# An attention and feed-forward kernel on one core: projection products split into four column groups of TensorE

## The chip, the cores and the metric

The kernel runs on one core of a Trainium2 chip. The core has TensorE (matrix products, PE in the profile; its weight loads are the row PEld), VectorE (DVE), ScalarE (ACT), GpSimd (POOL) and SyncE (SP), which issues most of the transfers. Each runs its own list of instructions, and they wait for each other by semaphores. The metric is the time of one execution on the device in microseconds (us), the median of several runs.

## The reference, cut to what matters

Four sequences of 1024 tokens with 512 channels go through cross-attention and a quantised feed-forward block, each behind a layer norm and added to its input:

```python
x = x + xattn(layernorm(x), ctx, Wq, bq, Wk, bk, Wv, bv, Wo, bo, 256, 768)
x = x + ffn(layernorm(x), clip_x, clip_down, w_gate, w_up, w_down)
# xattn: 16 heads of 32 channels
qh, kh, vh = heads(q @ Wq + bq), heads(kv @ Wk + bk), heads(kv @ Wv + bv)
scores = einsum('bhqd,bhkd->bhqk', qh, kh) * 32 ** -0.5
out = einsum('bhqk,bhkd->bhqd', softmax(where(mask, scores, -inf)), vh)
return merge(out) @ Wo + bo
```

The mask has three image chunks of 256 tokens that attend to themselves alone, and a text chunk of 256 tokens that attends to all image tokens and causally to itself. The change concerns the four products with Wq, Wk, Wv and Wo, which are 512x512 float32 matrices.

## The kernel before, in words

**Tiling.** The tokens of each sequence are cut into four blocks of 256 (`QB`), 16 blocks in all. Channels stand in four chunks of 128 partitions (`NCC`), and four heads of 32 channels share a chunk. A unit of attention is one block of queries, one chunk of heads (`g`), and one block of keys; an image block has one key block, a text block has four.

**The projections.** A `Job` makes the queries, or the keys and values, of one block. `rows` (L276) multiplies 128 columns of Wq or Wk, the stationary operand, by the transposed input `self.T` of 256 tokens, the moving operand, and sums over four chunks of the contraction in PSUM; it does this for two output chunks, `a`. ScalarE then moves the result with its bias to Q or K (L279). The values (L318) have 128 tokens of `self.T` as stationary operand and 512 columns of Wv as moving operand. `Output.step` (L603) multiplies 128 tokens of the attention output `oT` by 512 columns of Wo in the same way, and VectorE adds the result to the input (L582). Each call of one of these is a run of matmuls on TensorE that nothing else of TensorE interrupts. Near the end (`LATE`) some runs are made in halves. Line 288, the first block's keys, and line 777, the last block's output, are products of the same kind that have their own code.

**The attention.** `maxima` makes the scores (L421 image, L432 text), 32 rows of the array for each head; `weights` makes them again transposed, with the maximum subtracted by a small bfloat16 product (L479, L484); `values` multiplies the exponentials by V (L523) and by ones (L541), 32 columns of the array for each head:

```python
nc.tensor.matmul(
    av[rows_of(j), 0, cols], va[:, n, g * P + j * D : g * P + (j + 1) * D], u.pT[:, j, n, cols],
    start=..., stop=..., tile_position=(0, j * D), skip_group_check=True,
)
```

So the kernel already uses TensorE's array in three ways: whole (128 rows by 128 columns), as four row groups (32 rows by 128 columns), and as four column groups (128 rows by 32 columns).

**The order.** The attention phase runs under a hand-written order. In step `n` of the loop at L812 stand `maxima` of unit n, then one piece of projection or output work (`large`, L829), then `weights` of unit n-5 and `values` of unit n-6; where there is no such piece, `values` comes ahead of `weights`. A second piece of projection may follow at L879, at the end of the step. Semaphores are set by the framework from what each instruction reads and writes.

**Float32.** Each float32 matmul of the program is two passes in the profile, each a weight load and a matmul. The program has 5391 matmuls on TensorE; the profile has 9179 records of matmuls and 9201 of weight loads. The feed-forward part (L1038, L1129, L1141) has bfloat16 products of one pass.

Of the kernel before, what the change touches and what calls it, by code (L numbers as in the profile page):

```python
# [19 lines left out]
P = 128  # L20
B, N, C = 4, 1024, 512
NH, D = 16, 32
FF = 1408
NCC = C // P
# [18 lines left out]
def kernel(ctx: ExitStack, tc: tile.TileContext, x, kv, Wq, bq, Wk, bk, Wv, bv, Wo, bo, clip_x, clip_down, w_gate, w_up, w_down, out):  # L43
    nc = tc.nc
# [77 lines left out]
    with ExitStack() as actx:  # L122
# [35 lines left out]
        W = {name: p.tile([P, NCC, C], F32, tag=name, name=f"{name}_sb") for name, p in (("Wo", ap), ("Wk", wp), ("Wv", wp), ("Wq", wp))}  # L158

        idle = ps_mm.tile([P, 512], F32, tag="mm", name="idle")  # L160
        rhs = onesb.unsqueeze(1).to_broadcast([P, 4, P])
# [51 lines left out]

        early = [True]

        def bank(name):

            if early[0]:
                return ps_sc.tile([P, 2, 2, QB], F32, tag="sc", name=name).rearrange("p a b c -> p a (b c)")[:, 0, :]
            return ps_mm.tile([P, 512], F32, tag="mm", name=name)  # L220
# [16 lines left out]
        class Job:  # L237
# [8 lines left out]
            def run_small(self):  # L246
                if self.small == 0:
                    self.T = wk2.tile([P, NCC, QB], F32, tag="tT", name=f"{self.kind}T_{self.c}")
                i = self.small
                self.small += 1  # L250
                if self.c > 0:
                    src = spreads.pop(self.a)
                    nc.vector.transpose(self.T.rearrange("p c (k q) -> p k c q", q=D), src.rearrange("p k (e c) -> p k c e", c=NCC))
                    return

                if self.kind == "q":
                    while not ready.get(self.c):
                        background.popleft()()
                src = cb0 if self.kind == "kv" else xb0
                pt = bank(f"pt_{self.kind}_{self.c}_{i}").rearrange("p (a b) -> p a b", a=NCC)  # L260
                cols = src[:, i, :].rearrange("p (f k) -> p k f", k=NCC)
                for cc in range(NCC):
                    nc.tensor.transpose(pt[:, cc, :], cols[:, cc, :], ident)
                nc.scalar.copy(self.T[:, :, i * P : (i + 1) * P], pt)
                if i == 1 and self.kind == "kv":
                    columns_of_biases()
                elif i == 1:
                    next_queries(self.c)

            def rows(self, dst, w, b, scale, co, parts):  # L270

                pk = bank(f"pp_{self.kind}_{self.c}_{co}_{parts[0]}").rearrange("p (a q) -> p a q", a=2)
                for a in parts:
                    for ci in range(NCC):
                        lhs = W[w][:, ci, (co + a) * P : (co + a + 1) * P]
                        nc.tensor.matmul(pk[:, a, :], lhs, self.T[:, ci, :], start=(ci == 0), stop=(ci == NCC - 1))  # L276
                for a in parts:
                    bias = bqk[:, b + co + a : b + co + a + 1]
                    nc.scalar.activation(dst[:, co + a, :], pk[:, a, :], AF.Identity, bias=bias, scale=scale)  # L279
# [18 lines left out]
            def run_big(self, half=False):  # L298

                parts = (self.part,) if half or self.part else (0, 1)  # L300
                c, i = self.c, self.big
                first = parts[0] == 0
                if self.kind == "q":
                    if i == 0 and first:
                        Q[c] = qp.tile([P, NCC, QB], F32, tag="qT", name=f"qT_{c}")
                    self.rows(Q[c], "Wq", 0, QK_SCALE, 2 * i, parts)
                elif i < 2:
                    if i == 0 and first:
                        K[c] = kp.tile([P, NCC, QB], F32, tag="kT", name=f"kT_{c}")
                    self.rows(K[c], "Wk", NCC, 1.0, 2 * i, parts)  # L310
                else:
                    i -= 2
                    if i == 0 and first:
                        V[c] = kp.tile([P, 2, C], F32, tag="va", name=f"va_{c}")
                    cols = slice(parts[0] * QB, (parts[-1] + 1) * QB)
                    pv = bank(f"pv_{c}_{i}_{parts[0]}")
                    for ci in range(NCC):
                        nc.tensor.matmul(pv[:, cols], self.T[:, ci, i * P : (i + 1) * P], W["Wv"][:, ci, cols], start=(ci == 0), stop=(ci == NCC - 1))  # L318
                    nc.scalar.copy(V[c][:, i, cols], pv[:, cols])
                if parts[-1] == 1:  # L320
                    self.big += 1
                    self.part = 0
                else:
                    self.part = 1
                return len(parts)
# [56 lines left out]
        def rows_of(j):  # L382
            return slice(j * D, (j + 1) * D)
# [179 lines left out]
        class Output:  # L563
# [34 lines left out]
            def step(self, half=False):  # L598
                i = self.i
                cols = slice(self.part * QB, (self.part + 1) * QB) if half or self.part else slice(0, C)  # L600
                po = ps_mm.tile([P, 512], F32, tag="mm", name=f"po_{self.k.n}_{i}_{self.part}")
                for cc in range(NCC):
                    nc.tensor.matmul(po[:, cols], self.k.oT[:, cc, i * P : (i + 1) * P], W["Wo"][:, cc, cols], start=(cc == 0), stop=(cc == NCC - 1))  # L603
                statistics = self.take(po, i, cols)
                if statistics is None:
                    self.part = 1
                else:
                    background.appendleft(statistics)
                    self.part = 0
                    self.i += 1  # L610
# [287 lines left out]
        for i in range(2):  # L898
            cols = slice(i * P, (i + 1) * P)
# [298 lines left out]
```

## Time and profile before

| | |
|---|---|
| median of 3 runs | 1147.1 us (1145.67 to 1147.92) |
| the profiled execution | 1145.78 us, of which the span from first to last instruction is 1144.1 us |
| granted TensorE clock | 0.993 of full speed |
| TensorE busy | 1123.2 us, 98% of the span |
| weight loads busy | 655.7 us, 57% |
| VectorE, ScalarE, GpSimd busy | 784.0, 500.3, 549.3 us |
| matmul records of L276, L318, L603 | 992, 272, 280 |
| code fetched for TensorE (queue q8) | 72 packets of 16 KB |

The page of the profile gives the busy time of each engine, then the chain of work that ended last, followed back from the last instruction, then groups of instructions by line. A row such as `L276 PE MATMUL pp_q<-qT,Wq_sb 128*128 128x256 f32 x512 | 121.8, 390` reads: line 276, on TensorE, writes pp_q from qT and Wq_sb, 128 rows by 128 columns of the array, moving operand of 128x256 float32, 512 records, 121.8 us busy in all, 390 ns the mean of one. Matmuls overlap each other, so a mean of 390 ns is a time from start to end and not the spacing of two matmuls. In the timeline a row is a group of records in a row: its start, the time to the end of its last one, and their number.

### The profile page before, as it was taken

How to read it: one execution, taken by the hardware profiler on the slowest of the kernel's cores; microseconds unless marked ns; L12 is line 12 of the kernel's file. 1: busy time of each engine (PE TensorE's matmuls, PEld its weight loads, DVE VectorE, ACT ScalarE, POOL GpSimd, SP SyncE). 2: the span in 40 equal slices, each digit the busy share in tenths (PEclk: the TensorE clock that was granted, in tenths of full speed). 3: DMA queues.
4: the chain of work that ended last, by engine and by line, in shares of the span. 5: the costliest groups of instructions: out<-in, count | busy, mean ns of one | idle time of the engine just before them, and what ended most of it. 6: DMA issues, size and time to landing. Idle time of an engine off the chain costs nothing.

```text
span 1144.1 us, 22086 instructions
## 1 busy us (share of the span) xinstructions
PE 1123.2 (98%) x9179; PEld 655.7 (57%) x9201; DVE 784.0 (69%) x979; ACT 500.3 (44%) x700; POOL 549.3 (48%) x618
## 2 busy tenths in 40 slices
PE   9999999999999999999999999998999899999998
PEld 6666656575656656665646566665664344444344
DVE  2546676766577857567777656775676688877887
ACT  3334433343444434444433345544343466553553
POOL 1224546567664567775546569566763222110110
PEclk9999999999999999999999999999999899999999
DMA  7342213123222221331323122110222499310895
GB/s 257 111 127 63 61 48 101 48 85 92 80 61 75 73 78 57 92 114 24 86 66 86 40 73 79 46 50 26 85 67 75 133 282 292 80 38 11 303 388 191
DMA packets 117165, 118.50 MB, mean 104 GB/s; under 512 B 55548, under 2 KB 86536, under 8 KB 115656
## 3 DMA queue, kind: packets, MB, share of 16 engines
q1 hardware_dynamic: 111104, 83.26, 26.0%
q0 software_dynamic: 5648, 33.30, 7.8%
q8 instruction: 72, 1.18, 0.4%
q10 hardware_dynamic: 312, 0.53, 0.2%
q14 instruction: 29, 0.24, 0.1%
HBM read 71.57 MB, written 33.29 MB: 92 GB/s over the span
## 4 chain that ended last, share of the span: by engine, by line
PE 94%; DVE 2%; POOL 2%; ACT 1%; issue 1%; DMA 0%; DVEq 0%; POOLq 0%; ACTq 0%
PE pv L318 10%; PE po L603 10%; PE pp_q L276 10%; PE pp_kv L276 10%; PE av L523 9%; PE t L484 8%; PE pg L1038 7%; PE pu L1038 6%; PE s L432 6%; PE pd L1141 5%; PE s L421 5%; PE t L479 3%; PE av L541 3%; POOL sp L509 1%; PE pd L1129 1%
## 5 line engine op out<-in xcount | busy, mean ns | idle before, releaser
L489 ACT ACTIVATE pT<-t 128x1024 f32<-128x1024 f32 x224 | 217.1, 1021 | 193.8 <-PE t L484 186.4
L509 POOL TENSOR_TENSOR sp<-sp,pT 128x1024 f32<-128x1024 f32 x86 | 190.4, 2214 | 40.9 <-ACT pT L489 37.1
L443 DVE TENSOR_REDUCE nmh<-s 128x2 f32<-128x1024 f32 (+1 forms) x128 | 145.3, 1157 | 71.1 <-PE s L432 68.9
L509 POOL TENSOR_TENSOR sp<-pT 128x1024 f32<-128x1024 f32 x59 | 138.8, 2352 | 92.6 <-ACT pT L489 92.5
L425 DVE TENSOR_REDUCE nmh<-s 128x4 f32<-128x1024 f32 x96 | 112.7, 1215 | 101.2 <-PE s L421 101.2
L276 PE MATMUL pp_q<-qT,Wq_sb 128*128 128x256 f32 x512 | 121.8, 390 | 0.0
L318 PE MATMUL pv<-Wv_sb,kvT 128*128 128x512 f32 (+1 forms) x272 | 118.8, 579 | 0.0
L523 PE MATMUL av<-pT,va 128*32 128x256 f32 (+1 forms) x1792 | 116.5, 377 | 1.0 <-ACT avs L886 1.0
L484 PE MATMUL t<-qT,kT 32*128 32x256 f32 (+1 forms) x1792 | 113.0, 366 | 0.0
L603 PE MATMUL po<-Wo_sb,oT 128*128 128x512 f32 (+1 forms) x280 | 112.5, 544 | 0.2
L276 PE MATMUL pp_kv<-kvT,Wk_sb 128*128 128x256 f32 x480 | 111.5, 385 | 0.0
L556 DVE RECIPROCAL avs<-avs 128x256 f32<-128x256 f32 x63 | 109.8, 1742 | 0.0
L276 PEld LDWEIGHTS pp_q<-qT,Wq_sb 128*128 128x128 f32 x512 | 95.5, 192 | 23.1 <-issue 7.9
L276 PEld LDWEIGHTS pp_kv<-kvT,Wk_sb 128*128 128x128 f32 x480 | 88.8, 190 | 20.5 <-issue 7.6
L557 POOL TENSOR_TENSOR oT<-avs 128x256 f32<-128x256 f32 x63 | 46.0, 731 | 99.6 <-DVE avs L556 99.5
L484 PEld LDWEIGHTS t<-qT,kT 32*128 32x128 f32 x1792 | 88.1, 184 | 6.8
L1038 PE MATMUL pg<-xqT,wgT 128*128 128x512 bf16 x344 | 89.9, 381 | 1.1 <-DVE xqT L999 0.5
L1038 PE MATMUL pu<-xqT,wuT 128*128 128x512 bf16 x345 | 89.7, 380 | 0.4
L1044 ACT ACTIVATE silu<-pg,sg 128x512 f32<-128x512 f32 x88 | 60.0, 687 | 64.7 <-PE pg L1038 62.7
L1065 DVE SCALAR_TENSOR_TENSOR h<-pu,su,silu 128x512 f32<-128x512 f32 x88 | 65.4, 747 | 30.1 <-PE pu L1038 27.4
L318 PEld LDWEIGHTS pv<-Wv_sb,kvT 128*128 128x128 f32 x272 | 49.0, 189 | 54.4 <-issue 50.0
L432 PE MATMUL s<-kT,qT 32*128 32x256 f32 (+1 forms) x1024 | 76.3, 387 | 3.0 <-ACT pT L489 3.0
(186 smaller groups left out, 1415.3 us busy)
## 6 DMA issues: line engine op xcount, KB each, us to landing
xt<-x_d SPq DMA_DIRECT2D x16, 1024.0 KB, 6.3
h<-h_d POOLq DMA_DIRECT2D x3, 2816.0 KB, 13.4
xb<-in_x_dram SPq DMA_DIRECT2D x16, 512.0 KB, 3.8
xr<-in_x_dram SPq DMA_DIRECT2D x16, 512.0 KB, 3.8
x_d<-xr POOLq DMA_DIRECT2D x16, 512.0 KB, 3.8
spread_kv<-in_ctx_dram SPq DMA_DIRECT2D x60, 128.0 KB, 2.6
xn_d<-xb SPq DMA_DIRECT2D x15, 512.0 KB, 3.2
spread_q<-xn_d SPq DMA_DIRECT2D x60, 128.0 KB, 2.7
```

What stands on the lines that cost most here:

```text
L276: nc.tensor.matmul(pk[:, a, :], lhs, self.T[:, ci, :], start=(ci == 0), stop=(ci == NCC - 1))
L318: nc.tensor.matmul(pv[:, cols], self.T[:, ci, i * P : (i + 1) * P], W["Wv"][:, ci, cols], start=(ci == 0), stop=(ci == NCC - 1))
L425: nc.vector.tensor_reduce(nmh[:, h, :, :, 0], prs[h], AX.X, ALU.max, negate=True)
L432: nc.tensor.matmul(prs[j // 2][:, j % 2, kk, :w], q[rows_of(j), g, i * P : (i + 1) * P], K[k.keys[2 * half + kk]][rows_of(j), g, :w], star ...
L443: nc.vector.tensor_reduce(nmh[:, h, :, i, half], s[:, :, :n], AX.X, ALU.max, negate=True)
L484: nc.tensor.matmul(prs[j // 2][:, j % 2, n, cols], kc[rows_of(j), g, n * P : (n + 1) * P], q[rows_of(j), g, cols], start=False, stop=(n == 1))
L489: nc.scalar.activation(pT[:, 2 * h : 2 * h + 2], prs[h], AF.Exp)
L509: nc.gpsimd.tensor_tensor(sp[:, :, cols], a, pT[:, :, n, cols], ALU.add)
L523: nc.tensor.matmul(av[rows_of(j), 0, cols], va[:, n, g * P + j * D : g * P + (j + 1) * D], u.pT[:, j, n, cols], start=(u.part == 0 and n = ...
L556: nc.vector.reciprocal(avs[:, 1, :], avs[:, 1, :])
L603: nc.tensor.matmul(po[:, cols], self.k.oT[:, cc, i * P : (i + 1) * P], W["Wo"][:, cc, cols], start=(cc == 0), stop=(cc == NCC - 1))
L1038: nc.tensor.matmul(ps, w[:, cc, ic * P : (ic + 1) * P], qT[:, cc, :], start=(cc == 0), stop=(cc == NCC - 1))
```

## The change

A new function `column_groups` replaces one matmul of 128 stationary columns by four of 32, each at its own column group of the array and with its own 32 partitions of the result. Lines 276, 318 and 603 call it; lines 288, 198 and 777 stay as they are. The lines after 215 move by seven.

```diff
+        def column_groups(out, lhs, rhs, start, stop):
+
+            for j in range(4):
+                nc.tensor.matmul(
+                    out[rows_of(j)], lhs[:, rows_of(j)], rhs, start=start, stop=stop, tile_position=(0, j * D), skip_group_check=True
+                )
+
...
-                        nc.tensor.matmul(pk[:, a, :], lhs, self.T[:, ci, :], start=(ci == 0), stop=(ci == NCC - 1))
+                        column_groups(pk[:, a, :], lhs, self.T[:, ci, :], ci == 0, ci == NCC - 1)
...
-                        nc.tensor.matmul(pv[:, cols], self.T[:, ci, i * P : (i + 1) * P], W["Wv"][:, ci, cols], start=(ci == 0), stop=(ci == NCC - 1))
+                        column_groups(pv[:, cols], self.T[:, ci, i * P : (i + 1) * P], W["Wv"][:, ci, cols], ci == 0, ci == NCC - 1)
...
-                    nc.tensor.matmul(po[:, cols], self.k.oT[:, cc, i * P : (i + 1) * P], W["Wo"][:, cc, cols], start=(cc == 0), stop=(cc == NCC - 1))
+                    column_groups(po[:, cols], self.k.oT[:, cc, i * P : (i + 1) * P], W["Wo"][:, cc, cols], cc == 0, cc == NCC - 1)
```

The program then has 7707 matmuls on TensorE where it had 5391. The order of the work on every engine is the same.

## The prediction

> **What bounds the kernel now.** I read the engines' busy times first, then the chain of work that ended last, both on the page.
>
> ```profile
> PE 1123.2 (98%) x9179; PEld 655.7 (57%) x9201; DVE 784.0 (69%) x979; ACT 500.3 (44%) x700; POOL 549.3 (48%) x618
> PE 94%; DVE 2%; POOL 2%; ACT 1%; issue 1%; DMA 0%; DVEq 0%; POOLq 0%; ACTq 0%
> ```
>
> TensorE is the bound: 94% of the chain is its own work, and the next engine is busy 69%. A microsecond of TensorE is a microsecond of the end. But busy time does not say how fast its passes follow each other, so I went on to the groups by shape, and then to the timeline of one step.
>
> ```profile
> L276 PE MATMUL pp_q<-qT,Wq_sb 128*128 128x256 f32 x512 | 121.8, 390 | 0.0
> L523 PE MATMUL av<-pT,va 128*32 128x256 f32 x1664 | 113.0, 385 | 1.0 <-ACT avs L886 1.0
> L276 PEld LDWEIGHTS pp_q<-qT,Wq_sb 128*128 128x128 f32 x512 | 95.5, 192 | 23.1 <-issue 7.9 <-ACT pT L489 0.8 <-DVE avs L556 0.8
> L523 PEld LDWEIGHTS av<-pT,va 128*32 128x32 f32 x1792 | 46.7, 109 | 54.6 <-issue 23.3 <-ACT kT L279 3.7 <-ACT qT L279 3.3
> ```
>
> These hold both forms: the product as it is (L276, 128 columns), and the form it is to have, in use already for the values (L523, 32 columns, at the same width of 256). One pass lasts as long in either, 390 and 385 ns. A weight load is 192 ns for 128 columns and 109 ns for 32.
>
> ```profile
> 298.27 3.72 PE L276 MATMUL pp_kv<-kvT,Wk_sb 128*128 128x256 f32 x16
> 301.92 0.39 PE L479 MATMUL t<-nmT,onesb 2*128 2x512 bf16 x4
> 302.15 1.03 PE L484 MATMUL t<-qT,kT 32*128 32x256 f32 x16
> 303.11 1.07 PE L523 MATMUL av<-pT,va 128*32 128x256 f32 x16
> 304.00 0.61 PE L541 MATMUL av<-sp,ones 128*32 128x256 f32 x8
> 304.54 1.15 PE L421 MATMUL s<-kT,qT 32*128 32x256 f32 x16
> 305.62 1.55 PE L603 MATMUL po<-Wo_sb,oT 128*128 128x512 f32 x3
> ```
>
> Starts minus starts give real costs. L541 has 8 records in 0.54 us: two sets of four that run at once in the four groups, 0.216 each, and 0.11 to drain before L421. L523 has 16 records in 0.89 us: four sets of 0.216 and 0.024 more. L276 has 16 records, one at a time, in 3.65 us: 16 x 0.216 is 3.456, and 0.194 is left. In the single records, 0.104 of that is between the first pass and the second (320 ns apart, all later ones 216), while the first weight load isn't covered; 0.09 to 0.10 is the drain at the end, before L479 with its other use of the array. So a set of four 32-column passes costs what one 128-column pass costs, and the two forms differ only at the ends of a run.
>
> **The change, part by part.**
>
> *Steady part.* The 992 records of L276, 272 of L318 and 280 of L603 become sets of four. The sets cost 0.216 us at width 256, as L523 shows. At width 512 the trace has no 32-column float32 pass: between 0.43 (twice L523's; the wide pass at L603 has 0.43 too) and four in turn, 1.7 us. I take 0.43, since L479's four 512-wide passes start within 10 ns of each other. Change: 0.
>
> *Start of a run.* Coming from row groups, the second pass follows with 0.104 us more than its spacing (113 runs in the trace, all 101 to 155 ns), because a load of 190 ns stands open. With 32 columns it is 0.024 (L523). Gain 0.080 a run.
>
> *End of a run.* The four passes of a set start over 20 ns (7 ns apart in L523's records), so the last ends 20 ns later. The drain is 0.112 behind a column-group run (L541 to L421) and 0.093 to 0.096 behind a wide one. Loss 0.02 a run. Net 0.06 us for each run between row groups; the trace has 112, together 6.7 us.
>
> *A change of mode that goes away.* In 18 runs the projection comes right behind `values`, which is in column groups already:
>
> ```profile
> 200.67 0.61 PE L523 MATMUL av<-pT,va 128*32 128x256 f32 x8
> 201.22 3.72 PE L276 MATMUL pp_kv<-kvT,Wk_sb 128*128 128x256 f32 x16
> 204.87 0.94 PE L432 MATMUL s<-kT,qT 32*128 32x256 f32 x16
> ```
>
> Two sets need 0.43, and L276 starts after 0.55: a drain of 0.113. Then 0.104 for the first load. Both go, as between L523 and L541, which follow each other in the same spacing. Less 0.02 at the end: 0.2 x 18 = 3.6 us. The four other runs stand at the start between wide ones or elsewhere: nothing.
>
> *Instructions.* 2316 more float32 matmuls are 4632 more weight loads and as many passes on TensorE, 9264 on 18,380. Their code is 0.59 MB on the 1.18 MB of q8, which arrives in 16 KB packets (256 instructions), one in 13 us now and one in about 7 us in a step with L276; a packet takes 0.9 to 1.4 us, so the fetch stays hidden if it runs ahead at all. What is not free is their issue. A step with L276 is 7.14 us (291.20 to 298.34 in the chain), and will hold 64 + 60 pairs of load and pass, 248 instructions: 28.8 ns each. Now they come at half that rate, with the queue filling during each wide run. How fast can the sequencer feed? The trace bounds it twice. First, the densest stretch:
>
> ```profile
> 717.65 0.39 PE L479 MATMUL t<-nmT,onesb 2*128 2x512 bf16 x4
> 717.88 1.03 PE L484 MATMUL t<-qT,kT 32*128 32x256 f32 x16
> 718.84 0.86 PE L523 MATMUL av<-pT,va 128*32 128x256 f32 x16
> 719.51 0.61 PE L541 MATMUL av<-sp,ones 128*32 128x256 f32 x8
> 719.94 0.83 PE L541 MATMUL av<-pT,ones 128*32 128x256 f32 x16
> 720.71 1.15 PE L432 MATMUL s<-kT,qT 32*128 32x256 f32 x16
> ```
>
> 76 pairs in 3.83 us (to the last start), with no gap but the drains. At L1141 a semaphore wait of TensorE's sequencer is recorded 16 loads ahead of the array, so some 34 of the 152 instructions were queued before, and the rest came in at 32 ns or faster. Second, at 7.8 us the queue is empty: the sequencer ends one recorded wait at 7.779, issues two loads and two passes (L183), and begins its next wait at 7.894. Four in 115 ns is 29 ns at most; two waits with nothing between them elsewhere are 54 to 60 ns apart, so the four took some 15 each. I take 15, and keep 29 to 31 as the slow end.
>
> [...]
>
> *Other engines.* Their instructions and order are the same. ScalarE's moves (L279, L319) and VectorE's add (L582) start up to 0.06 earlier. TensorE's semaphore waits as separate instructions rise from 60 to 79, each 51 ns of the sequencer, behind a queue some 16 pairs deep: nothing; without that cover, 19 x 0.11 = 2 us.
>
> Sum: 6.7 + 3.6 = 10.3 us. Against the profiled execution 1145.8 - 10.3 = 1135.5. The median of the runs stands 1.3 us above that execution, so 1136.8.
>
> **The rivals.**
>
> *The sequencer becomes the bound (slower).* Place: the steps with L276, with eight instructions for each 0.216 us. It decides above 28.8 ns an instruction. For it: at 7.80 the first load and the first pass behind an empty queue are 31 ns apart. At 31 ns a step is 7.69, 0.55 us more than now; 62 of them lose 34 us, the other runs (about 72, half the extra density because they are 512 wide) still gain some 6: 1175 us. At 29.5 ns it would be about even. Against it: the 115 ns above.
>
> *The four groups don't run at once.* In all column-group rows of before the four moving operands differ; here they are one. If reading it together cost even a tenth, the 427 us of these lines (1104 passes of 0.216, 440 of 0.43) would grow by 43: 1180. Against it: L523 reads four streams over all 128 partitions already.
>
> *The gain is hidden.* If TensorE came to wait for others as much earlier as it gets ahead, 1147. For it: four waits of TensorE's sequencer between 730 and 804 us end 30 ns after VectorE's signal. Against it: TensorE had 0.55 to 1.06 us of queued work each time.
>
> **How the numbers follow.** My forecast has 0.73, with 1132 to 1142 of its own: the low end if the exit cost is also smaller, the high end if half the gain per run is lost. The hidden gain has 0.06, the sequencer as bound 0.14 (half of that only mildly, below 1165), the groups in each other's way 0.07. The range is 1132 to 1165, which takes in forecast, hidden gain and a mild bound. A change below 0.2% (2.3 us) can't be told from none. Faster by more 0.74, within 0.06, slower 0.20.
>
> **What would show it.** Right: sets of L276 and L318 0.216 and 0.43 apart, the second set 24 ns late and not 104, no drain between L523 and a following projection, runs of 3.59 us where they were 3.65. Wrong: sets of L276 further apart than 0.216 towards a run's end, or steps of more than 7.14 us, which is the sequencer; a pass of the split lines longer than 0.38 us, or the second to fourth of a set starting late, which is the shared operand; gaps ahead of L421 or L432 that name VectorE, which is the hidden gain.

## The result, and the profile after

The changed kernel takes 1139.43 us, the median of four runs (1138.92 to 1140.27), against 1146.89 us (1145.67 to 1147.92) for the kernel before. The ratio is 0.9936, with a 95% interval from 0.9919 to 0.9953. That is 7.5 us less; the forecast was 10.3 less. The profiled execution took 1139.15 us with a span of 1137.4, against 1145.78 and 1144.1, which is 6.6 us less. All lines behind 215 have moved by seven: L219 is the matmul of the new function, L428 and L439 are the scores, L486 and L491 the transposed scores, L530 and L548 the products with V and with ones.

From the page of the kernel after, busy times, the code queue, the chain, and two groups:

```profile
PE 1116.0 (98%) x13811; PEld 562.5 (49%) x13833; DVE 784.9 (69%) x979; ACT 500.1 (44%) x700; POOL 551.5 (48%) x618
q8 instruction: 108, 1.77, 0.7%
PE 91%; DVE 3%; DMA 2%; POOL 2%; ACT 1%; issue 1%; DVEq 0%; POOLq 0%; ACTq 0%
L219 PE MATMUL pp_q<-qT,Wq_sb 128*32 128x256 f32 x2048 | 119.3, 383 | 0.0
L219 PEld LDWEIGHTS pp_q<-qT,Wq_sb 128*32 128x32 f32 x2048 | 63.7, 110 | 48.8 <-issue 8.7
```

TensorE is still the bound. There are four times as many records of the query projection, and each lasts 383 ns where it was 390; busy time counts overlapping records once, so it went from 121.8 to 119.3 us. The load of 32 columns takes 110 ns where 128 took 192.

The timeline of the step that the prediction dissected, in the kernel after (start, time to the end of the last record, records):

```profile
296.36 3.66 PE L219 MATMUL pp_kv<-kvT,Wk_sb 128*32 128x256 f32 x64
299.95 0.39 PE L486 MATMUL t<-nmT,onesb 2*128 2x512 bf16 x4
300.18 1.03 PE L491 MATMUL t<-qT,kT 32*128 32x256 f32 x16
301.14 1.07 PE L530 MATMUL av<-pT,va 128*32 128x256 f32 x16
302.03 0.61 PE L548 MATMUL av<-sp,ones 128*32 128x256 f32 x8
302.57 1.15 PE L428 MATMUL s<-kT,qT 32*128 32x256 f32 x16
```

The run of L219 now reaches L486 after 3.59 us, where L276 reached L479 after 3.65. Everything behind it has the spacing of before. And this is a projection behind `values` in the kernel after:

```profile
199.25 1.07 PE L530 MATMUL av<-pT,va 128*32 128x256 f32 x16
200.14 3.64 PE L219 MATMUL pp_kv<-kvT,Wk_sb 128*32 128x256 f32 x64
203.70 0.94 PE L439 MATMUL s<-kT,qT 32*128 32x256 f32 x16
```

Four sets of L530 take 0.89 us to L219, 0.864 and the first load of 0.024: no drain is left between them. L219 itself takes 3.56 us, where L276 took 3.65 in this place.

**Where the 6.6 us of the profiled pair arise.** Start times of the same TensorE work in both traces, after minus before:

| place | before, us | after minus before, us |
|---|---|---|
| scores s of the first units | 30.10 | +0.63 |
| next values pv | 44.06 | +0.96 |
| in steady work | 68.6 | +0.98 |
| attention's end, pm_x | 895.39 | -8.20 |
| feed-forward, pu | 904.96 | -7.38 |
| its end | 1139.04 | -6.62 |

From 68.6 to 895 us the change gains 9.2 us. It loses 1.0 ahead of that and 1.6 behind it. The projections that it edits lie in the middle; the two losses lie where the prediction had put nothing.

The middle has a loss of its own. Added up run by run, the split runs there, with the `values` runs right ahead of some of them, are 10.2 us shorter; 1.0 us of that comes back, nearly all of it between 690 and 850 us, where TensorE now waits for other engines, or waits for longer. One such place, before:

```profile
756.86 0.59 PE L479 MATMUL t<-nmT,onesb 2*128 2x512 bf16 x4
757.08 1.02 PE L484 MATMUL t<-qT,kT 32*128 32x256 f32 x16
```

and after:

```profile
749.70 0.76 PE L486 MATMUL t<-nmT,onesb 2*128 2x512 bf16 x4
750.08 1.04 PE L491 MATMUL t<-qT,kT 32*128 32x256 f32 x16
```

L484 follows L479 after 0.22 us, as elsewhere; L491 follows L486 after 0.38. In both traces the third pass of the first line waits for VectorE's reduction `nmh` and starts 0.05 us behind its end; before, that cost TensorE nothing. Three such places lose 0.37 us, and waits for GpSimd (L548) and ScalarE (L439) grow from 1.37 to 1.50 and from 3.00 to 3.19 us.

The experiments ask three things: is the gain made of the parts that the prediction named, what are the losses at the start and behind the attention, and how far away was the rival of the instruction feed?

### The profile page after: what moved, and what is told of

Its sections match the earlier page's. It is cut to its first block, busy times and chain, and to the rows that moved or that the text cites. A ratio compares the mean times of both kernels' runs of the same rounds, so it can differ in the third digit from the quotient of the medians.

```text
span 1137.4 us, 31369 instructions
## 1 busy us (share of the span) xinstructions
PE 1116.0 (98%) x13811; PEld 562.5 (49%) x13833; DVE 784.9 (69%) x979; ACT 500.1 (44%) x700; POOL 551.5 (48%) x618
## 3 DMA queue, kind: packets, MB, share of 16 engines
q8 instruction: 108, 1.77, 0.7%
## 4 chain that ended last, share of the span: by engine, by line
PE 91%; DVE 3%; DMA 2%; POOL 2%; ACT 1%; issue 1%; DVEq 0%; POOLq 0%; ACTq 0%
PE pv L219 10%; PE po L219 9%; PE pp_kv L219 9%; PE pp_q L219 9%; PE av L530 9%; PE t L491 8%; PE pg L1045 7%; PE pu L1045 7%; PE s L439 6%; PE s L428 5%; PE t L486 3%; PE av L548 3%; PE pd L1148 2%; DMA xt<-x_d 2%; POOL sp L516 2%
## 5 line engine op out<-in xcount | busy, mean ns | idle before, releaser
L432 DVE TENSOR_REDUCE nmh<-s 128x4 f32<-128x1024 f32 x96 | 112.8, 1216 | 97.7 <-PE s L428 95.5
L219 PE MATMUL pp_q<-qT,Wq_sb 128*32 128x256 f32 x2048 | 119.3, 383 | 0.0
L530 PE MATMUL av<-pT,va 128*32 128x256 f32 (+1 forms) x1792 | 116.5, 377 | 1.0 <-ACT avs L893 1.0
L219 PE MATMUL pv<-Wv_sb,kvT 128*32 128x512 f32 (+1 forms) x1088 | 116.9, 570 | 0.0
L491 PE MATMUL t<-qT,kT 32*128 32x256 f32 (+1 forms) x1792 | 113.4, 367 | 0.0
L219 PE MATMUL po<-Wo_sb,oT 128*32 128x512 f32 (+1 forms) x1120 | 110.3, 534 | 0.3
L219 PE MATMUL pp_kv<-kvT,Wk_sb 128*32 128x256 f32 x1920 | 109.6, 380 | 0.0
L491 PEld LDWEIGHTS t<-qT,kT 32*128 32x128 f32 x1792 | 88.3, 185 | 7.0
L219 PEld LDWEIGHTS pp_q<-qT,Wq_sb 128*32 128x32 f32 x2048 | 63.7, 110 | 48.8 <-issue 8.7
L219 PEld LDWEIGHTS pp_kv<-kvT,Wk_sb 128*32 128x32 f32 x1920 | 60.1, 110 | 44.1 <-issue 5.4
L439 PE MATMUL s<-kT,qT 32*128 32x256 f32 (+1 forms) x1024 | 76.4, 387 | 3.2 <-ACT pT L496 3.2
L530 PEld LDWEIGHTS av<-pT,va 128*32 128x32 f32 x1792 | 46.8, 109 | 54.5 <-issue 23.7
```

Source lines behind the costliest of these rows:

```text
L219: nc.tensor.matmul(out[rows_of(j)], lhs[:, rows_of(j)], rhs, start=start, stop=stop, tile_position=(0, j * D), skip_group_check=True)
L432: nc.vector.tensor_reduce(nmh[:, h, :, :, 0], prs[h], AX.X, ALU.max, negate=True)
L439: nc.tensor.matmul(prs[j // 2][:, j % 2, kk, :w], q[rows_of(j), g, i * P : (i + 1) * P], K[k.keys[2 * half + kk]][rows_of(j), g, :w], star ...
L491: nc.tensor.matmul(prs[j // 2][:, j % 2, n, cols], kc[rows_of(j), g, n * P : (n + 1) * P], q[rows_of(j), g, cols], start=False, stop=(n == 1))
L530: nc.tensor.matmul(av[rows_of(j), 0, cols], va[:, n, g * P + j * D : g * P + (j + 1) * D], u.pT[:, j, n, cols], start=(u.part == 0 and n = ...
```

## The experiments

### One part alone: only Wq and Wk split, only Wv and Wo split

```diff
-column_groups(pv[:, cols], self.T[:, ci, i * P : (i + 1) * P], W["Wv"][:, ci, cols], ci == 0, ci == NCC - 1)
+nc.tensor.matmul(pv[:, cols], self.T[:, ci, i * P : (i + 1) * P], W["Wv"][:, ci, cols], start=(ci == 0), stop=(ci == NCC - 1))
...
-column_groups(po[:, cols], self.k.oT[:, cc, i * P : (i + 1) * P], W["Wo"][:, cc, cols], cc == 0, cc == NCC - 1)
+nc.tensor.matmul(po[:, cols], self.k.oT[:, cc, i * P : (i + 1) * P], W["Wo"][:, cc, cols], start=(cc == 0), stop=(cc == NCC - 1))
```

The second kernel undoes the call in `rows` instead, so that pv and po alone are split.

> Only the products with Wq and Wk (line 276 of before) are split. Theory (the gain lies at the ends of runs, 0.06 us for a run between row groups and 0.2 us for one right behind the values product): some 50 runs of 0.06 and 12 of 0.2, 5.4 us, less about 0.6 lost at the start of the kernel, so the product that starts the feed-forward part (pm_x) begins at about 890.6 us where before had 895.39 and the full change 887.20; passes in the runs stay 216 ns apart, run 3.59 us. Rival (the sequencer's feed takes part of the gain in these dense steps): sets further apart than 216 ns towards the end of a run, pm_x later than 892.

> Only the products with Wv and Wo (lines 318 and 603 of before) are split. Theory: some 60 runs of 0.06 and 6 of 0.2, 4.8 us, less about 0.4 at the start: pm_x begins at about 891.0. Half as dense in instructions as the other, so the rival (the feed) gives the same here; the two halves together then make up 9.2 us of the 8.2 that the full change had at that point if they don't depend on each other.

Wq and Wk alone: 1143.51 us, ratio 0.9969 (0.9958 to 0.9981). Wv and Wo alone: 1145.61, ratio 0.9978 (0.9967 to 0.999). In each trace the split runs have the new length (3.593 us for pp, 3.573 for pv and po) and the others the old one (3.653 and 3.633). So the gain per run is additive. The times are less so: 3.8 and 1.7 us of gain against before in the same comparison, 5.5 together, where both at once have 7.5.

The start of pm_x missed too. It begins at 894.03 and 893.71 us, where 890.6 and 891.0 were expected; for Wq and Wk, a start behind 892 was to speak for the instruction feed. The feed isn't the reason: the sets stay 216 ns apart to the end of a run. Up to 700 us the two parts do add up: from 68.6 us on they gain 4.2 and 3.2 us, and both at once 7.5. What is missing in these traces lies in two places. One is at 783 us, where TensorE waits for ScalarE in every kernel and the clock is then granted at half: for 3.41 us before and after, for 6.83 in each of the two parts. The scores behind this wait, before and with Wq and Wk alone:

```profile
786.73 0.92 PE L432 MATMUL s<-kT,qT 32*128 32x256 f32 x12 [3.00 <-ACT pT L489]
784.07 1.65 PE L439 MATMUL s<-kT,qT 32*128 32x256 f32 x12 [3.82 <-ACT pT L496]
```

The wait is longer, and the twelve records take 1.65 us instead of 0.92. Up to the next `values`, at 792.34 us before, Wq and Wk alone lose 2.3 us in this place and Wv and Wo alone 1.4, both at once 0.1. (Not every execution loses as much: the profiled one of Wq and Wk alone took 1146.11 us, 2.6 above the median.) The other place lies in the first 50 us. Before, and with Wq and Wk alone:

```profile
42.99 1.15 PE L421 MATMUL s<-kT,qT 32*128 32x256 f32 x16
```

```profile
39.31 3.70 PE L325 MATMUL pv<-Wv_sb,kvT 128*128 128x512 f32 x8
42.94 0.70 PE L428 MATMUL s<-kT,qT 32*128 32x256 f32 x4
43.98 1.13 PE L428 MATMUL s<-kT,qT 32*128 32x256 f32 x12 [0.34 <-DVE nmh L432]
45.04 1.12 PE L325 MATMUL pv<-Wv_sb,kvT 128*128 128x512 f32 x2
```

Up to 42.94 this kernel stands where the one before does (42.99). Then the scores, which before came as 16 records in a row, stop after four and wait for VectorE's reduction of earlier scores. That costs 1.0 us, and it has nothing to do with TensorE's products.

### The first products left whole

The whole loss at the start looked at first like one cause, the prediction's "four other runs". The first transposes and keys (L270, L295) still use the whole array, so products that were whole beside them now change the array's use. The timelines of the first values, before:

```profile
15.28 3.60 PE L318 MATMUL pv<-Wv_sb,kvT 128*128 128x512 f32 x8
18.72 1.11 PE L263 MATMUL pt_q<-ident,xb 128*128 128x128 f32 x8
19.67 3.60 PE L318 MATMUL pv<-Wv_sb,kvT 128*128 128x512 f32 x8
23.10 1.24 PE L276 MATMUL pp_q<-qT,Wq_sb 128*128 128x256 f32 x5
```

and after:

```profile
15.52 3.64 PE L219 MATMUL pv<-Wv_sb,kvT 128*32 128x512 f32 x32
19.09 1.23 PE L270 MATMUL pt_q<-ident,xb 128*128 128x128 f32 x8
20.25 3.64 PE L219 MATMUL pv<-Wv_sb,kvT 128*32 128x512 f32 x32
23.71 0.61 PE L219 MATMUL pp_q<-qT,Wq_sb 128*32 128x256 f32 x8
```

Against the start of pv, pt_q comes 3.57 us later instead of 3.44, and the next pv 1.16 behind pt_q instead of 0.95. With the start of the first pv, 0.24 late of which 0.14 was there already, this makes the 0.6 us by 23.7 us.

```diff
 def column_groups(out, lhs, rhs, start, stop):
+    if early[0]:
+        nc.tensor.matmul(out, lhs, rhs, start=start, stop=stop)
+        return
     for j in range(4):
```

> The full change, but the runs made while the flag early is set (before the loop, and a few in its first five steps) stay whole, 128 columns. Theory (the start of the kernel lost about 1 us because split runs there stand between whole-array transposes and products, so that the split adds mode changes): the lag against before at the projection that starts at 68.6 us in before falls from 0.98 us to 0.3 or less, and pm_x begins near 886.4 instead of 887.20. Rival (the lag is an accident of transfers or of the clock): it stays near 1 us.

These steps went: 38.28 before stands at 38.33 here. But the time is 1139.82 us, ratio 0.9927 (0.9904 to 0.9949), the same as with the full change, and the lag at 68.6 us is +1.53. The scores behind 42.98 stopped and waited as they do in the trace above, so that pv of 44.06 came at 45.18. The expectation of at most 0.3 us of lag failed, and so did that of pm_x near 886.4: it came at 889.29, with 1.7 us lost at 783 us, where this kernel too had 6.83 us of half clock. The mode changes are one cause of 0.4 us; there is a second, of about 1 us.

### Is the second cause an accident of the run?

The kernel before was run again, unchanged.

> The kernel before, profiled once more. The profile of the full change lags 0.98 us at the projection that before starts at 68.6 us, and the kernel with whole early runs (e3) lags as much although its start is the one of before. Theory: the lag is an accident of the start of the run that was profiled, so this profile also lags, by 0.7 to 1.5 us at that place, with no product split. Rival: it starts that projection within 0.3 us of 68.6 again, and the lag belongs to the changed kernels.

It took 1145.74 us, and its TensorE work stands within 0.04 us of the first trace throughout (pv at 44.09, pm_x at 895.38). The lag belongs to the changed kernels.

### What makes VectorE late: the code fetch

The waiting chain goes back from the scores to VectorE's reduction, from there to its transpose of `spread_q`, and from there to the four transfers that bring `spread_q`. In these the traces differ, together with the moments at which a 16 KB packet of TensorE's code (queue q8) was under way, read from the transfer records:

| kernel | first issue of spread_q, us | nearest code packet starts, us | issue to transpose, us |
|---|---|---|---|
| before | 35.54 | 45.6 | 4.20 |
| before again | 35.57 | 44.9 | 4.08 |
| all split | 36.23 | 35.7 | 4.43 |
| Wq, Wk alone | 35.58 | 37.2 | 5.22 |
| Wv, Wo alone | 36.17 | 36.8 | 4.90 |
| first products whole | 35.45 | 36.3 | 5.36 |

With more instructions there are more packets (108 in the fully split kernel, 72 before), and one of them falls on this transfer. A packet that starts 0.6 to 1.6 us behind the first issue goes with 0.7 to 1.2 us more. One kernel of those below belongs to these too (5.25 us); in all others but the next, the nearest packet starts 0.5 us or more ahead of the first issue or 5.9 us or more behind it, and the time is 4.1 to 4.6 us. To tell it from everything else that the split changes, the last experiment moves the packets in the kernel before, whose products stay whole: 66 short idle matmuls ahead of the first work instead of 14 long ones, which adds 104 instructions and brings the packet of 45.6 us forward. Idle matmuls have no part in the output.

```diff
-for _ in range(14):
-    nc.tensor.matmul(idle.rearrange("p (a b) -> p a b", a=4), onesb, rhs, start=True, stop=True)
+for _ in range(66):
+    nc.tensor.matmul(idle[:, :96], onesb, onesb[:, :96], start=True, stop=True)
```

> The kernel before, no product split, with 66 short idle matmuls at its start where it has 14 long ones: 104 more instructions on TensorE in about the same time, so that its second 16 KB packet of code (queue q8) starts near 36.4 us instead of 45.6. Theory (a packet of code that starts while the four transfers spread_q are issued near 36 us delays them, and with them VectorE's transpose of the queries and the scores behind it; in the changed kernels it falls there): the transpose starts 4.9 to 5.4 us after the first of the four is issued, where before has 4.1 to 4.3, and the projection that starts at 44.06 us in before is late by 0.3 to 1.1 us against the work ahead of it. Rival (the two only happen together): 4.1 to 4.3 us and no lag.

The packet came at 35.23 us, earlier than the 36.4 that were aimed at, the first issue at 35.63. VectorE's timeline in this kernel:

```profile
40.61 2.02 DVE L253 STREAM_TRANSPOSE qT<-spread_q 128x1024 f32<-128x1024 f32 x1 [7.14 <-DMA spread_q<-xn_d]
```

and in the kernel before:

```profile
39.74 2.02 DVE L253 STREAM_TRANSPOSE qT<-spread_q 128x1024 f32<-128x1024 f32 x1 [6.11 <-DMA spread_q<-xn_d]
```

Issue to transpose is 4.98 us instead of 4.20. TensorE's timeline, with moved packets:

```profile
39.19 3.70 PE L318 MATMUL pv<-Wv_sb,kvT 128*128 128x512 f32 x8
42.83 0.70 PE L421 MATMUL s<-kT,qT 32*128 32x256 f32 x4
43.79 1.13 PE L421 MATMUL s<-kT,qT 32*128 32x256 f32 x12 [0.27 <-DVE nmh L425]
44.85 1.55 PE L318 MATMUL pv<-Wv_sb,kvT 128*128 128x512 f32 x3
```

TensorE reaches the scores 0.16 us earlier than before, stops after four records, and is 0.79 us late at pv. The whole time, 1148.57 us in one run, tells nothing, since the kernel before took 1156.33 in its one run beside it. Against the span of before, the span of 1146.9 is 2.8 us longer: 0.8 in this place, 0.8 at 783 us (6.83 us of half clock again), 1.0 in the last products. So a kernel in which no product is split shows, in one trace, the same late transfer and the same stop when its code packet is brought to that place. No trace shows what holds the transfer up, and no rule from the packet's moment to the delay: packets that start 0.4 to 0.5 us ahead of the first issue went with 0.8 us here, with 0.2 in the fully split kernel, and with none in the last series of it below (4.13 us). In the profile of the change the transfer cost 0.2, on top of a VectorE that was 0.7 late by its own earlier work; together these made the scores wait 0.45.

### The loss behind the attention: the clock

From 895 us on the order of work is the feed-forward block's, which the change doesn't touch. Its start, before, with the granted clock (PEclk) in two windows:

```profile
895.00:900.00 5.00, 3.46 (x18) 1.76 (x19) 4.00 (x11) 1.65 (x3) 1.62 (x3) 0.68 0.79 249
900.00:905.00 5.00, 4.26 (x18) 1.94 (x18) 1.91 (x7) 1.39 (x2) 0.38 (x1) 0.64 0.65 213
```

and the same place after, 7 us earlier (columns: window, length, busy time and records of PE, PEld, DVE, ACT and POOL, granted clock, DMA share, GB/s):

```profile
888.00:893.00 5.00, 3.29 (x20) 1.87 (x20) 4.41 (x12) 1.24 (x2) 1.40 (x2) 0.72 0.79 239
893.00:898.00 5.00, 4.75 (x13) 1.82 (x14) 1.09 (x4) 1.61 (x3) 0.61 (x1) 0.60 0.49 186
```

In both, TensorE idles while the maximum of x is reduced and the input quantised, and the clock is then granted at half for a stretch: 896.8 to 903.6 us before, 890.2 to 897.0 after, 0.50 of full speed over either. In these two traces each stretch that ends within the span has a length of 3.41 us or twice that, and within a trace they begin a whole number of 3.413 us apart: before, 32 and 80 of them behind the one at 787.53 us; after, 32 and 79 behind the one at 780.98. What sets these times no run shows. But the stretch moved less than the work: it comes 6.5 us earlier after the change, the first pu 8.2 (902.88 to 894.68). Before, half clock ended 0.7 us behind that start, and the products then followed each other 216 ns apart; after, it lasted 2.4 us into them, 427 ns apart:

```profile
893.83 1.06 PE L1045 MATMUL pg<-xqT,wgT 128*128 128x512 bf16 x2 [0.22 <-issue]
894.68 1.91 PE L1045 MATMUL pu<-xqT,wuT 128*128 128x512 bf16 x4
896.39 1.35 PE L1045 MATMUL pg<-xqT,wgT 128*128 128x512 bf16 x4
897.58 1.03 PE L1045 MATMUL pu<-xqT,wuT 128*128 128x512 bf16 x4
```

The first four pu take 1.71 us to the next pg, where in the kernel before they took 1.21 (902.88 to 904.09), and the next pg 1.19 instead of 0.87. The second idle place, at 1050 to 1060 us, is the same again: 3.41 us of half clock before, 6.83 after, and 0.6 us lost up to 1072 us, 0.2 of it within the first products behind it. The remaining 0.1 lies in the last products. In the kernel with the first products whole there was no half clock behind the attention, and it made up 1.5 us against before in that place.

If half clock is the cause, both kernels with TensorE kept busy in these places must show the gain without this loss. The edit adds idle matmuls; the computation stays as it is.

```diff
 # idle_tail, ahead of pm_x
-for _ in range(12):
+for _ in range(19):
...
 # idle_x
-for _ in range(4):
+for _ in range(10):
...
+idle = ps_x.tile([P, C], F32, tag="pm", name="idle_h0")
+for _ in range(14):
+    nc.tensor.matmul(idle.rearrange("p (a b) -> p a b", a=4), identb, identb.unsqueeze(1).to_broadcast([P, 4, P]), start=True, stop=True)
 scale_h, rcp_h = tensor_scale(hmax, "h", ps_x)
...
 # idle_h
-for _ in range(4):
+for _ in range(7):
```

> The full change, with more idle matmuls where TensorE waits: 19 instead of 12 ahead of pm_x, 10 instead of 4 behind it, 14 new ones ahead of pm_h and 7 instead of 4 behind it. Theory (1.1 us of the gain was lost because TensorE's clock was at half for longer after the start of the feed-forward part and after pm_h than it was in the run of before): no stretch at half clock after pm_x or pm_h, the lag steps there go away and the time is 1 to 2.5 us shorter than with the full change, 1137 to 1138.5. Rival (the steps are not the clock's): same time as the full change, 1139.4, or longer by the idle work.

> The kernel before with the idle matmuls of e7 and no split. Theory (the split's gain of about 10 us is in the attention part whatever the clock does, and the runs of the full change just met more stretches at half clock): 10 us (9.3 to 10.7) slower than the same with the split (e11), so about 1145.5, and 0.5 to 2.5 us faster than before. Rival (the split's gain is the 7.5 us that the medians show): 7.5 us slower than e11, about 1143.

> The kernel of e7 (the full change with more idle matmuls) once more, beside e10. Theory and rival: 1135.5 again; the difference to e10 tells them apart, 10 us or 7.5 us. The profile shows no half clock after pm_x and pm_h.

| kernel | as it is, us | with idle matmuls, us |
|---|---|---|
| before | 1146.44 | 1144.13 (1143.01 to 1145.35), ratio 0.9976 (0.9967 to 0.9984) |
| all split | 1139.43 | 1135.35 (1134.19 to 1136.1), ratio to before 0.9904 (0.9891 to 0.9918) |
| difference | 7.5 in its own comparison | 8.8 |

An earlier series of the split kernel with idle matmuls had 1135.51, 1.5 us below the range expected. Its profiled run took 1144.22, with a stop of 5.5 us within the feed-forward products at 950.7 us, whose cause stays open, and half clock behind it; the other five took 1134.69 to 1135.95. The windows, taken from the second series:

```profile
885.00:890.00 5.00, 4.49 (x23) 1.97 (x21) 3.71 (x11) 2.38 (x4) 1.62 (x3) 1.00 0.63 207
890.00:895.00 5.00, 4.03 (x25) 2.13 (x27) 2.99 (x9) 1.85 (x4) 1.12 (x3) 1.00 0.71 247
1045.00:1050.00 5.00, 4.31 (x21) 1.88 (x19) 4.11 (x10) 0.00 (x0) 0.00 (x0) 1.00 0.64 195
```

The clock is 1.00 through both places, and 0.998 over the span in both kernels with idle matmuls; the 3.41 us of half clock at 783 us stay in both. The split kernel gains 4.1 us by them and the whole one 2.3, so half clock cost the split one 1.8 us more; by the two differences it is 1.3 (the kernel before had medians of 1146.89 and 1146.44 in the two comparisons). The medians alone don't carry this, since the intervals of 7.5 and 8.8 overlap; but the pair of traces without idle matmuls has it too, 0.8 at the first place and 0.6 at the second, and in the pair with them neither place loses anything.

The 8.8 lies between the 10 (9.3 to 10.7) that was expected and the 7.5 of its rival. The traces of the two account for it: the split kernel is 0.6 us late at 68.6 us and 8.8 early at pm_x, so 9.3 arise in the attention, against 9.2 without the idle matmuls. Its runs are 10.2 us shorter there too, and 0.9 comes back in the same waits behind 690 us. The spans are 1141.8 and 1132.5, 9.3 apart; the last half microsecond of that is one more wait of the whole kernel for ScalarE in the last products, and no work of the split. The sum of 10.3, less the four runs that stand ahead of 68.6 us (0.24), is 10.06.

The split kernel with idle matmuls is the fastest of this study, 11.1 us below the kernel before in the same comparison. With the first products whole as well, it is no faster:

> The full change with both: the early runs left whole and the idle matmuls of e7. Theory: the two add up, 1.5 to 3.3 us below the full change, about 1137. Rival (neither is a cause): 1139.4.

1136.13 us (1136.03 to 1138.02), ratio 0.9913 (0.9899 to 0.9927). This kernel too met a code packet (transfer 5.25 us), which takes back what the whole products gave.

### Two groups of 64 columns

```diff
-for j in range(4):
+for j in range(2):
+    half = slice(j * 2 * D, (j + 1) * 2 * D)
     nc.tensor.matmul(
-        out[rows_of(j)], lhs[:, rows_of(j)], rhs, start=start, stop=stop, tile_position=(0, j * D), skip_group_check=True
+        out[half], lhs[:, half], rhs, start=start, stop=stop, tile_position=(0, j * 2 * D), skip_group_check=True
     )
```

> Two column groups of 64 columns instead of four of 32, in all three products. Theory: the first weight load of a run stands open for a time between 0.024 (32 columns) and 0.104 us (128), about 0.05, and two passes start within 7 ns instead of four within 20: 0.05 to 0.06 us gained in each of some 112 runs, nearly as with four groups. Behind the values product (32 columns) there are two answers: if going from 32 to 64 columns is no change of mode for the array, the 18 runs gain as with four groups and the time is about 1140; if it drains, they gain only 0.06 and the time is about 1142.

1142.38 us, ratio 0.997 (0.9958 to 0.9982). This separates the two terms of the prediction's sum. A run between row groups is 3.607 us long (3.653 whole, 3.593 in four groups): the shorter open load (138 ns for 64 columns, 110 for 32 and 192 for 128) is had almost in full. But behind `values` the change of use stays:

```profile
200.03 1.07 PE L531 MATMUL av<-pT,va 128*32 128x256 f32 x16
201.03 3.67 PE L220 MATMUL pp_kv<-kvT,Wk_sb 128*64 128x256 f32 x32
204.63 0.94 PE L440 MATMUL s<-kT,qT 32*128 32x256 f32 x16
```

Four sets of L531 take 1.00 us to L220, as before the change, and not 0.89. From groups of 32 columns to groups of 64 the drain of 0.11 us stays.

### How close was the instruction feed?

Each split product of Wq and Wk was made in two moving halves of 128 tokens, so that eight instructions stand for each 0.108 us of the array instead of 0.216. (The sums of pp are not the reference's in this kernel; the passes, loads and their order are those of the edit.)

```diff
-column_groups(pk[:, a, :], lhs, self.T[:, ci, :], ci == 0, ci == NCC - 1)
+for h in range(2):
+    m = slice(h * P, (h + 1) * P)
+    column_groups(pk[:, a, m], lhs, self.T[:, ci, m], ci == 0, ci == NCC - 1)
```

> The full change, and each split product with Wq and Wk also cut into two moving halves of 128 tokens: twice the loads and passes of half the length, so a set of four pairs (eight instructions) takes 108 ns of the array. This measures how fast TensorE's sequencer feeds. Theory (about 15 ns an instruction): sets 108 to 120 ns apart, runs of 3.6 to 4.0 us, 1139 to 1163 us. Rival (29 to 31 ns an instruction): sets some 240 ns apart once the queue is empty, runs of 6 to 7.8 us, 1290 to 1400 us.

```profile
299.11 3.70 PE L219 MATMUL pp_kv<-kvT,Wk_sb 128*32 128x128 f32 x128
302.74 0.40 PE L488 MATMUL t<-nmT,onesb 2*128 2x512 bf16 x4
```

The run holds 128 passes and 128 loads and takes 3.63 us, against 3.59 with half of them; the sets follow each other 108 to 109 ns apart to the end of the run. That is 13.5 ns for an instruction or less, kept up over 256 of them, more than any queue that the traces show (16 loads ahead of the array, at L1141 in the kernel before). The feed would bind the change's steps above 28.8 ns; it is at least twice as fast. The whole kernel took 1144.16 us in one run.

### The order of the four groups

The same four times 32 columns, but all passes of one group ahead of those of the next:

```diff
-for ci in range(NCC):
-    column_groups(pk[:, a, :], lhs, self.T[:, ci, :], ci == 0, ci == NCC - 1)
+for j in range(4):
+    for ci in range(NCC):
+        lhs = W[w][:, ci, (co + a) * P + j * D : (co + a) * P + (j + 1) * D]
+        nc.tensor.matmul(pk[rows_of(j), a, :], lhs, self.T[:, ci, :], ..., tile_position=(0, j * D), skip_group_check=True)
```

> In the products with Wq and Wk the loop over the four column groups stands outside the loop over the contraction, so that eight passes of one group follow each other in the program; the work is the same. Theory (four groups run at once only as far as TensorE looks ahead, some 16 to 20 pairs of load and pass): two groups at once, a run of 6.9 us instead of 3.59, some 62 runs, about 1345 us. Rival (it looks ahead over more than 32 pairs, or has a queue for each group): no change, 1139.

```profile
347.64 8.17 PE L284 MATMUL pp_kv<-kvT,Wk_sb 128*32 128x256 f32 x64
355.74 0.39 PE L489 MATMUL t<-nmT,onesb 2*128 2x512 bf16 x4
```

1414.37 us in one run. A run takes 8.10 us instead of 3.59, more than the 6.9 expected. In the single records the first pass of a group starts with the fifth of the eight passes of the group ahead, and at each of the seven seams four passes overlap: 64 less 28 is 36 passes in turn, and 36 x 0.216 is 7.78, plus 0.32 at the ends. The half runs fit as well: 32 less 12, 20 x 0.216 = 4.32, and 4.53 measured. So in this kernel passes started no more than some four places ahead of their turn in the program; in the change, where the four groups are neighbours there, the same passes take 3.59 us.

## Why the prediction was right, and where it was off

**Steady part, 0: right.** Sets of L219 are 216 ns apart at width 256 and 429 at 512. The 512-wide split pass, which before had no row, costs what the wide one cost; the rival of the four groups in each other's way has no trace in it.

**Start and end of a run, +0.080 and -0.020: right to the nanosecond that the trace can tell.** First to second pass 320 to 240 ns (534 to 454 at width 512); first pass of the last set to the next use 312 to 332 (525 to 545), since the four passes start over 20 ns. A run between row groups is 0.060 shorter, and with two groups of 64 columns 0.046, for first loads of 110 and 138 ns where the whole one has 192.

**The change of mode behind `values`, 0.2 x 18: right.** The run of V (four sets) is 0.113 shorter (1.001 to 0.888) and the projection behind it 0.084 (3.651 to 3.567): 0.197 each. With two groups of 64 the drain doesn't go away (1.00).

**Instructions: right in the feed, wrong in "the fetch stays hidden".** The estimate of 15 ns an instruction stands: 13.5 or less. Code grew to 108 packets and 1.77 MB as worked out, and no wait of TensorE in the trace was found to name it (the only one put down to issue, 0.22 us, is there before as well). But the fetch has other neighbours than TensorE: where a packet started 0.6 to 1.6 us behind the first issue of `spread_q`, VectorE's transpose came 0.7 to 1.2 us later, and the scores stood behind it. In the profile of the change this is a small part of the 1 us at the start; with Wq and Wk alone, and with the first products whole, it is most of it.

**"The four other runs: nothing": mis-sized.** Beside the whole-array transposes and keys of the first 24 us the split products bring mode changes that were not there, 0.4 to 0.5 us together. They hit the end, since TensorE is the bound there too (busy 22.57 of the first 24 us in both traces), and VectorE's next work is late with it.

**Left out altogether: the clock.** The prediction took the part behind the attention as moved, not changed. Half clock there took 1.3 to 1.8 us more than in the kernel before by the two pairs with and without idle matmuls, 1.4 by the traces.

**"The gain is hidden": true in a small part.** The prediction gave this rival 0.06 for the whole gain and put nothing for a part of it. It had looked at four waits for VectorE between 730 and 804 us, which are at L432 and L421, and found 0.55 us or more of queued work at each. The waits that grew stand partly at other lines in the same stretch (L486, three times), where in the trace of before VectorE's signal already came only 0.05 us ahead of the pass. With those for ScalarE and GpSimd they took 0.9 to 1.0 us.

So of the 10.06 us beyond the start the runs gave 10.2; 1.0 came back in waits, 1.0 was lost at the start (0.6 in the pair with idle matmuls), and 1.6 behind the attention, nearly all of it to half clock: 6.6 us in the profiled pair. The forecast of 1136.8 missed 1139.43 by these, and by the 0.2 us between two medians of before. Its mechanism and every term for the steady runs were right. That the time also lies within the 1132 to 1142 of its likeliest case is in part luck: that range allowed for less gain in each run, and the runs gave all of it; what was lost came from the start, the waits and the clock, which the sum had at nothing.

## What to carry to other kernels

Where a product of 128 stationary columns stood between products in another tiling of the array, four groups of 32 cost nothing in the steady part here (216 ns a set, as for a wide pass); the gain was a shorter open first load (0.060 us a run), and the drain as well where the run ahead had the same groups (0.197), so weigh the neighbours before the product. Keep the four groups next to each other in the program (3.59 us a run; one behind the other, 8.10). Look for waits that end just in time now: 1.0 of the 10.2 us gained on TensorE came back there. When a change moves later work by some microseconds, look at what the clock and the code packets meet at the new time, and compare kernels with those places kept busy before judging a change of half a per cent.

## What the runs showed of the hardware that was not expected

- In the half-width kernel TensorE took 32-column float32 loads and passes at 13.5 ns an instruction or faster over 256 instructions.
- With one column group behind the other, passes of the next group started no more than about four passes ahead of their place in the program: 8.10 us for a run that takes 3.59 with the groups interleaved.
- From groups of 32 columns to groups of 64 there was 0.11 us of drain (1.00 us for four sets, 0.89 where groups of 32 followed).
- A 16 KB packet of code beside a short transfer went with up to 1.2 us of delay in it, 0.8 (one trace) in a kernel that was changed in nothing but its idle matmuls.
- Stretches of half clock began a whole number of 3.413 us apart in the trace of before (32 and 80) and in that of after (32 and 79). Keeping TensorE busy in the same two idle places gained the kernel before 2.3 us and the split one 3.6 to 4.1; what sets the beginning and the length of a stretch was not shown.
